# A segment sum by two matmul passes: a quarter of the late chunk products in two float32r parts

## The chip, the cores and the metric

The kernel runs on one core of one Trainium2 chip. The metric is the device time of one execution in microseconds (us), less is better. The core has five engines with a queue each: TensorE (PE in the profile, with its weight loads as PEld), VectorE (DVE), ScalarE (ACT), GpSimd (POOL) and SyncE (SP). Each engine works through its own queue in order. DMA transfers are started from the queues of SP, ACT and POOL.

## The reference, cut to what matters

```
def _L0_gnn_ref(x, edge_index, edge_features, global_feat, W_c, b_c, W1, b1, W2, b2, W3, b3):
    row = edge_index[0]
    edge_aggr = jnp.zeros((n, HIDDEN)).at[row].add(edge_features)
    combined = concatenate([x, edge_aggr, global_expand]) @ W_c + b_c
    h = softplus(combined @ W1 + b1)
    h = softplus(h @ W2 + b2)
    return h @ W3 + b3
x = layernorm(x + _L0_gnn_ref(x, stack([src, dst]), edge_attr_128, ...))
```

There are 206,250 edge rows of 128 float32 numbers and 6,250 nodes. An edge row is added to the row of its node `src`, and the `src` come in no order. The sum over the edges, `edge_aggr`, is nearly all of the work; the three small layers and the layer norm follow per node.

## The kernel before, in words

The sum is made in two passes over the edges, which run at the same time, the second behind the first.

- **Sort.** The nodes are cut into 32 buckets of 196 (`BL`). The edges lie in 1,692 columns of 122 rows, two columns make a pair (846 pairs), up to three pairs make a piece. For each column DVE and PE work out which place in its column each edge gets (`slot`), a 0/1 matrix `sort_hot` is made from it (every second piece by one comparison on DVE, L1137; the others on ACT by six `Abs`, L1140, and one `Relu`, L1142), PE multiplies the edge rows by it (`gather`, L1153, tile `sorted`), ACT copies the result out of PSUM (`settle`, L1165, tile `pairs`), and POOL writes each pair to its places in DRAM with one indirect DMA (`scatter_row`, L1182, tensor `rows_by`). Gaps between the places are filled with rows of -1 by DMAs from a tile `fill`.
- **Sum.** `rows_by` is read back in chunks of 128 rows, all of one bucket or of two neighbours. A load on SP's queue brings up to 8 chunks into one of 6 buffers (`chunks`). Its chunks are worked on in units of up to four (`HALF`). DVE makes a 0/1 matrix `hot` of 128 rows by 196 nodes for each chunk of a unit (`match`, L990), and PE multiplies the chunk's rows by it in float32 (`product`, L1013): the 128x128 rows are the weights, `hot` streams past them, and the result adds up in a PSUM tile `part`. When a group of chunks is through, DVE adds `part` to `sums_t` (L1036).
- **Node layers.** In 13 tiles of up to 512 nodes: PE L1356 and L1357 (first layer, from `x_t` and `sums_t`), ACT L1367, L1368, L1373 (softplus), DVE L1381, PE L1360 (second layer), PE L1395 (third), DVE L1403 to L1410 (sum with x and its statistics), then the norm.

The order on PE, DVE, ACT and SP is written out by a planner in the kernel. Every step gets a time in planned microseconds: pair k is scattered at `FIRST + SCATTER * k`, and its gather, settle, comparisons and loads lie fixed distances ahead (`GATHERED`, `SETTLED`, `COMPARED`, `LOADED`). `sum_steps` gives each unit the time of its match and of its product: a match may stand 2 units ahead of the products (`TOGETHER`), after the last scatter 4 (`AT_END`). Steps are then issued in order of these times. The planned end of the scatters is `ends[-1]`, 24 + 1.3 x 846 = 1123.8. Steps of the sum that are planned later than that are kept as `rest`, and the node layers take them in between their own steps: up to `FIRST_STEPS` = 9 of them ahead of a tile's second and third layer, those still needed for the next tile's first layer behind. I call what comes after the last scatter the tail.

A float32 matmul of this program stands in the profile as two MATMUL and two LDWEIGHTS: 1,758 chunks make 3,516 rows of L1013, and 1,692 columns 3,384 rows of L1153.

Of the kernel before, what the change touches and what calls it, by code (L numbers as in the profile page):

```python
# [7 lines left out]
F32 = mybir.dt.float32  # L8
BF16 = mybir.dt.bfloat16
# [5 lines left out]
ALU = mybir.AluOpType  # L15
# [36 lines left out]
FILL, DUE = 7, 8  # L52
# [11 lines left out]
SHARE, SPREAD = 2, 2.0  # L64
# [3 lines left out]
MATCHED, MULTIPLIED, RATE = 9.0, 1.5, 0.58  # L68
NODES = (3, 4)
# [77 lines left out]
def kernel(  # L147
# [144 lines left out]
    def sync_dma(out, in_):  # L292
        return nc.sync.dma_start(out, in_).ins
# [16 lines left out]
    hots = ctx.enter_context(tc.tile_pool(name="hots", bufs=6))  # L310
# [8 lines left out]
    with ExitStack() as phase:  # L319
        rows_p = phase.enter_context(tc.tile_pool(name="rows", bufs=ROWS))  # L320
        sort_p = phase.enter_context(tc.tile_pool(name="sort", bufs=3))
# [29 lines left out]
        def scratch(name):  # L351
            return per.tile([P, 4 * P], F32, name=name, bufs=1)
# [53 lines left out]
        def fill_rows():  # L406
# [10 lines left out]
            def some(due, b, n, lo, rows, k):  # L417
                to = rows_by.rearrange("(s j) c -> s j c", j=STRIDE * P)[b:b + n, lo:lo + rows * k, :]
                ins = sync_dma(to.rearrange("b (p k) c -> p b (k c)", k=k),
                               fill[:rows, :k * ROW].unsqueeze(1).to_broadcast([rows, n, k * ROW]))  # L420
                apart(ins, "direct", ["scatter"])
                fills.setdefault(due, []).append(ins)

            def doubtful(b, mixed):
                if mixed:
                    start, end, twice, room, per = ROOM * P, STRIDE * P, 2, MIXED_ROOM / 2, MIXED_PER
                else:
                    start, end, twice, room, per = 0, rooms[b] * P, 1, rooms[b], ROWS_PER[kind[b]]
                lo = start + twice * int(certain(mixed, gap_at, room, per))
                hi = end - twice * untouched(mixed, per)  # L430
                rows, k = min(((rows, -(-(hi - lo) // rows)) for rows in (96, 112, P)),
                              key=lambda e: (e[0] * e[1], -e[0]))
                assert k <= FILL and lo + rows * k <= end
                return lo, rows, k
# [451 lines left out]
        def sum_steps():  # L886
# [37 lines left out]
            chunks, hots_of, parts_of, met, begun = {}, {}, {}, {}, set()  # L924
# [54 lines left out]
            def match(n):  # L979
                j, a, e = units_of[n]  # L980
                hot = hots.tile([P, HALF, BL], F32, name="hot")
                hots_of[n] = hot
                q = a
                while q < e:
                    lo = hi = place_in(j, q)
                    step, m = 1, 1
                    while q + m < e and place_in(j, q + m) > hi and (m == 1 or place_in(j, q + m) == hi + step):
                        step, hi = place_in(j, q + m) - hi, place_in(j, q + m)
                        m += 1
                    nc.vector.tensor_tensor(  # L990
                        hot[:, q - a:q - a + m],
                        chunks[j][:, lo:hi + 1:step, D:W].to_broadcast([P, m, BL]),
                        iota_ps.unsqueeze(1).to_broadcast([P, m, BL]), op=ALU.is_equal)
                    q += m
# [3 lines left out]
            def product(n):  # L998
# [9 lines left out]
                for q in range(a, e):  # L1008
# [4 lines left out]
                    nc.tensor.matmul(part[:, b - base_of[v], :], t[:, place_in(j, q), :D], hot[:, q - a],  # L1013
                                     start=first, stop=last)
# [26 lines left out]
            opened = -1  # L1041
            for n, (j, a, e) in enumerate(units_of):
# [11 lines left out]
                found.append((match_at[n], len(found), lambda n=n: match(n)))  # L1054
                found.append((product_at[n], len(found), lambda n=n: product(n)))
# [561 lines left out]
```

## Time and profile before

| | |
|---|---|
| median of 3 runs | 1289.03 us (1283.15 to 1290.0) |
| the profiled execution | 1289.92 us, its span 1288.2 us |
| busy, of the span | PE 91%, PEld 86%, DVE 80%, ACT 78%, POOL 68% |
| scatters | 846, the first at 22.1 us, the last starts at 1127.05 us |
| TensorE clock granted, mean | 0.962 |

A row of the groups reads: line, engine, operation, output and inputs, partitions x elements, count | busy us, mean ns of one | idle time of the engine ahead of it, and what ended the idle time. A row of the timeline: start us, length us, engine, line, operation, count. A row of the windows: the stretch, then for each engine its busy us and in brackets the number of instructions. Matmuls overlap each other, so that the distance between two starts is what one of a series costs, not its mean length.

### The profile page before, as it was taken

The numbers are of one execution on the slowest core, as the hardware profiler recorded it, in microseconds if no ns is written. First come the engines' busy times: TensorE is split into PE (matmuls) and PEld (weight loads), VectorE is DVE, ScalarE is ACT, GpSimd is POOL, SyncE is SP. The second block draws the span as 40 slices with busy tenths as digits, with TensorE's granted clock in tenths as the row PEclk, the third lists the DMA queues.
The fourth block names the chain that finished last, engine by engine and source line by source line (L and its number), as shares of the span: only waits on it lengthen the run. The fifth ranks groups of instructions, "written<-read, shape, count | busy, mean of one in ns | idle before, by whom it ended". The sixth has DMA issues, their size and how long they took to land.

```text
span 1288.2 us, 26304 instructions
## 1 busy us (share of the span) xinstructions
PE 1167.7 (91%) x8617; PEld 1111.8 (86%) x8617; DVE 1027.6 (80%) x2260; ACT 1003.9 (78%) x2335; POOL 880.9 (68%) x915
## 2 busy tenths in 40 slices
PE   5778898888998998999899999999999999899893
PEld 5667788877988898989899999999999999898772
DVE  7868977888789977899878887789876767687784
ACT  5897987899687888977998888988899999403343
POOL 2777777777577776776777777777777777750334
PEclk9788998989999998999999999999999999999996
DMA  6789998899999997997999999999999999874421
GB/s 248 240 296 347 344 334 288 305 344 355 339 327 331 362 330 278 319 325 246 322 309 309 323 336 328 345 313 335 316 350 334 369 336 363 288 218 140 140 75 53
DMA packets 174636, 381.96 MB, mean 297 GB/s; under 512 B 27546, under 2 KB 118626, under 8 KB 160670
## 3 DMA queue, kind: packets, MB, share of 16 engines
q1 hardware_dynamic: 130751, 260.70, 61.2%
q0 software_dynamic: 41328, 115.65, 23.1%
q10 hardware_dynamic: 2415, 3.85, 0.9%
q8 instruction: 72, 1.18, 0.4%
q14 instruction: 70, 0.57, 0.1%
HBM read 242.47 MB, written 142.20 MB: 299 GB/s over the span
## 4 chain that ended last, share of the span: by engine, by line
PE 65%; DVE 12%; ACT 8%; DMA 7%; issue 4%; POOL 3%; SPq 0%; ACTq 0%; DVEq 0%; POOLq 0%
PE part L1013 37%; PE sorted L1153 21%; ACT pairs L1165 4%; DMA rows_by<-pairs,pair 4%; POOL rows_by L1182 3%; ACT sort_hot L1140 3%; DMA chunks<-rows_by 3%; DVE hot L990 2%; DVE past L727 1%; PE small L557 1%; PE small L559 1%; ACT sort_hot L1142 1%; DVE sort_hot L1137 1%; DVE sums_t L1036 1%; PE small L1395 1%
## 5 line engine op out<-in xcount | busy, mean ns | idle before, releaser
L1182 POOL DMA_INDIRECT rows_by<-pairs,pair x846 | 828.1, 979 | 298.3 <-issue 202.8
L1013 PE MATMUL part<-hot,chunks 128*128 128x196 f32 x3516 | 675.1, 335 | 13.2 <-DVE sums_t L1036 9.9
L1165 ACT COPY pairs<-sorted 64x387 f32<-64x387 f32 (+2 forms) x1144 | 542.6, 474 | 118.8 <-PE sorted L1153 95.7
L1013 PEld LDWEIGHTS part<-hot,chunks 128*128 128x128 f32 x3516 | 582.0, 193 | 21.9 <-DVE sums_t L1036 11.3
L1153 PE MATMUL sorted<-rows,sort_hot 122*128 122x129 f32 x3384 | 498.5, 288 | 44.5 <-ACT sort_hot L1142 32.0
L1153 PEld LDWEIGHTS sorted<-rows,sort_hot 122*128 122x128 f32 x3384 | 457.6, 199 | 53.5 <-ACT sort_hot L1142 36.3
L990 DVE TENSOR_TENSOR hot<-chunks,both_ps 128x784 f32<-128x784 f32 (+3 forms) x541 | 426.1, 809 | 9.2 <-DMA chunks<-rows_by 9.0
L1140 ACT ACTIVATE sort_hot<-plain,slot 122x128 f32<-122x128 f32 x840 | 292.8, 394 | 18.6 <-PE sorted L1153 6.3
L1036 DVE TENSOR_TENSOR sums_t<-sums_t,part 128x392 f32<-128x392 f32 (+1 forms) x262 | 143.5, 548 | 134.0 <-PE part L1013 133.0
L1137 DVE TENSOR_TENSOR sort_hot<-slot,both_ps 122x768 f32<-122x768 f32 x143 | 134.5, 940 | 1.9 <-PE sorted L1153 1.0
L1142 ACT ACTIVATE sort_hot<-sort_hot 122x768 f32<-122x768 f32 x143 | 118.6, 830 | 3.9
L1437 POOL TENSOR_SCALAR y<-y,mv,rs 128x128 f32<-128x128 f32 x40 | 31.1, 785 | 93.8 <-DVE rs L1425 93.5
L576 DVE TENSOR_REDUCE slot<-small 122x16 f32<-122x512 f32 (+2 forms) x109 | 72.9, 668 | 21.5 <-PE small L559 20.7
L1367 ACT ACTIVATE away<-sorted,z_bias 128x512 f32<-128x512 f32 (+2 forms) x13 | 8.5, 656 | 72.9 <-PE sorted L1357 72.9
L498 DVE TENSOR_TENSOR pair_ib<-pair_block,plain 122x512 bf16<-122x512 bf16 (+2 forms) x157 | 63.4, 411 | 0.2
L557 PE MATMUL small<-pair_ib,half 122*122 122x512 bf16 (+2 forms) x109 | 43.3, 398 | 7.6 <-DVE slot L576 7.5
L742 PEld LDWEIGHTS <-past 128*128 128x128 f16 x424 | 25.4, 100 | 17.9 <-DVE past L727 12.7
L727 DVE TENSOR_TENSOR past<-both_ps,starts 128x512 f16<-128x512 f32 (+1 forms) x61 | 39.8, 664 | 1.2 <-PE small L742 0.9
L742 PE MATMUL small<-jump,past 128*128 128x56 f16 (+3 forms) x424 | 29.4, 190 | 11.8 <-DVE past L727 8.4
L559 PEld LDWEIGHTS <-starts_h 128*122 128x122 bf16 x236 | 25.3, 148 | 11.9 <-issue 7.7
L1114 ACT COPY rows<-pair_i 122x16 f32<-122x16 f32 x106 | 22.2, 209 | 17.0 <-DMA rows<-in_edge 16.4
L727 DVE TENSOR_TENSOR past<-both_ps,starts_late 128x512 f16<-128x512 f32 (+2 forms) x49 | 32.3, 661 | 0.0
(163 smaller groups left out, 515.6 us busy)
## 6 DMA issues: line engine op xcount, KB each, us to landing
rows<-in_edge SPq DMA_DIRECT2D x105, 1032.0 KB
chunks<-rows_by SPq DMA_DIRECT2D x362, 136.0 KB
chunks<-rows_by SPq DMA_DIRECT2D x203, 204.0 KB
chunks<-rows_by SPq DMA_DIRECT2D x75, 272.0 KB
rows_by<-pairs,pair POOLq DMA_INDIRECT x846
rows_by<-fill SPq DMA_DIRECT2D x10, 1249.5 KB
rows_by<-fill SPq DMA_DIRECT2D x10, 714.0 KB
chunks<-rows_by SPq DMA_DIRECT2D x13, 408.0 KB
```

The costliest lines, as they stand in the source:

```text
L498: nc.vector.tensor_tensor(ib, cols.unsqueeze(2).to_broadcast([PN, m, SB, QUAD]), bucket_at[:PN].unsqueeze(1).to_broadcast([PN, m, SB, QUAD ...
L576: nc.vector.tensor_reduce(to, of, axis=mybir.AxisListType.X, op=ALU.max)
L727: nc.vector.tensor_tensor(past[:, :, a:b], twice_ps[:KB].unsqueeze(1).unsqueeze(1).to_broadcast([KB, 2, b - a, P // 2]), own["starts"][:, ...
L990: nc.vector.tensor_tensor(hot[:, q - a:q - a + m], chunks[j][:, lo:hi + 1:step, D:W].to_broadcast([P, m, BL]), iota_ps.unsqueeze(1).to_bro ...
L1013: nc.tensor.matmul(part[:, b - base_of[v], :], t[:, place_in(j, q), :D], hot[:, q - a], start=first, stop=last)
L1036: nc.vector.tensor_add(here, here, of)
L1137: return [lambda: nc.vector.tensor_tensor(hot[:PN, :2 * m], slot[:PN, at:at + 2 * m].unsqueeze(2).to_broadcast([PN, 2 * m, P]), slot_ps[:P ...
L1140: return [lambda j=j: nc.scalar.activation(hot[:PN, j], by_slot[:PN], AF.Abs, bias=slot[:PN, at + j:at + j + 1], scale=-1.0) for j in rang ...
L1142: for j in range(2 * m)] + [lambda: nc.scalar.activation(hot[:PN, :2 * m], hot[:PN, :2 * m], AF.Relu, bias=1.0, scale=-1.0)]
L1153: nc.tensor.matmul(out[:, j, :], hot[:PN, at], rows_at[col // LOAD_COLS][:PN, col % LOAD_COLS, :], start=True, stop=True)
L1165: nc.scalar.copy(sets_at[i][64 * n:64 * n + 64, lo:lo + m, h, :W], out[64 * h:64 * h + 64, :m, :])
L1182: s = nc.gpsimd.indirect_dma_start(out=dst, out_offset=bass.IndirectOffsetOnAxis(ap=at, axis=0), in_=rows[:, j].rearrange("p a b -> p (a b ...
```

## The change

- **Two float32r parts.** From planned time 650 on, every fourth unit (after the last scatter every third) that has more than two chunks, lies in one run of its load, and is not planned between 30 ahead of the last scatter and 12 behind it, becomes `fine`. ACT copies its rows into a tile `high` as float32r (`high`), 4 planned us ahead of the product; DVE subtracts that from the rows and writes the remainder over them as float32r (`low`), 1.5 ahead; and PE makes two float32r products for each chunk where one float32 product was, `high` by `hot` and remainder by `hot`. There are two buffers for `high`. 76 units with 266 chunks become fine: 55 units (185 chunks) ahead of the last `gather`, 21 units (81 chunks) behind it.
- **Comparisons earlier.** `SPREAD` goes from 2.0 to 4.5: the comparisons of the sort on ACT start 17.5 + 4.5 = 22 planned us ahead of the scatter instead of 19.5, and `sort_hot` gets 4 buffers instead of 3.
- **Room.** `hot` gets 5 buffers instead of 6. `fill` holds 4 rows instead of 7, so that 12 fills become two DMAs each, and the scratch tiles of `node_codes` are halved.

```
-FILL, DUE = 7, 8
+FILL, DUE = 4, 8
-SHARE, SPREAD = 2, 2.0
+SHARE, SPREAD = 2, 4.5
+FINE_FROM, FINE_EVERY, HIGHS, COARSE = 650.0, (4, 3), 2, (-30.0, 12.0)
-    hots = ctx.enter_context(tc.tile_pool(name="hots", bufs=6))
+    hots = ctx.enter_context(tc.tile_pool(name="hots", bufs=5))
-        sort_p = phase.enter_context(tc.tile_pool(name="sort", bufs=3))
+        sort_p = phase.enter_context(tc.tile_pool(name="sort", bufs=4))
...
+                for a in range(0, k, FILL):
+                    w = min(FILL, k - a) * ROW
+                    ins = sync_dma(to[:, :, a * ROW:a * ROW + w],
+                                   fill[:rows, :w].unsqueeze(1).to_broadcast([rows, n, w]))
...
+            def high(n):
+                high_of[n] = sums_p.tile([P, HALF, D], F32R, name="high", bufs=HIGHS)
+                for to, at, m in runs_of(n):
+                    nc.scalar.copy(high_of[n][:, to], chunks[units_of[n][0]][:, at, :D])
+
+            def low(n):
+                for to, at, m in runs_of(n):
+                    rows = chunks[units_of[n][0]][:, at, :D]
+                    nc.vector.tensor_tensor(rows.bitcast(F32R), rows, high_of[n][:, to].bitcast(F32),
+                                            op=ALU.subtract)
...
-                    nc.tensor.matmul(part[:, b - base_of[v], :], t[:, place_in(j, q), :D], hot[:, q - a],
-                                     start=first, stop=last)
+                    rows, by = t[:, place_in(j, q), :D], hot[:, q - a]
+                    if n in fine:
+                        nc.tensor.matmul(part[:, b - base_of[v], :], high_of[n][:, q - a], by,
+                                         start=first, stop=False)
+                        nc.tensor.matmul(part[:, b - base_of[v], :], rows.bitcast(F32R), by,
+                                         start=False, stop=last)
+                    else:
+                        nc.tensor.matmul(part[:, b - base_of[v], :], rows, by.bitcast(F32),
+                                         start=first, stop=last)
...
+                since += 1
+                if (product_at[n] > FINE_FROM and since >= FINE_EVERY[product_at[n] > ends[-1]]
+                        and not COARSE[0] < product_at[n] - ends[-1] < COARSE[1] and e - a > 2 and len(runs_of(n)) == 1):
+                    since = 0
+                    fine.add(n)
+                    found.append((max(match_at[n], product_at[n] - 4.0), len(found), lambda n=n: high(n)))
+                    found.append((max(match_at[n] + 1.0, product_at[n] - 1.5), len(found), lambda n=n: low(n)))
```

The times of the other steps in the plan stay as they were: 1,471 of the 1,758 chunk products stand ahead of the sort's last matmul on PE before and after.

PE in the tail, around the first tile that reaches its third layer (L1395). Before:

```order
L1356 MATMUL sorted<-x_t,fold 128x512
L1357 MATMUL sorted<-sums_t,fold 128x512
L1013 MATMUL part<-hot,chunks 128x196 x10
L1360 MATMUL sorted<-h_13613,weights_sb 128x512
L1395 MATMUL small<-weights_sb,h_13615 128x128 x4
L1013 MATMUL part<-hot,chunks 128x196 x14
```

The same place after the change (the lines have moved: L1042 is the float32 product, L1037 and L1039 are the two float32r products of a chunk):

```order
L1392 MATMUL sorted<-x_t,fold 128x512
L1393 MATMUL sorted<-sums_t,fold 128x512
L1042 MATMUL part<-hot,chunks 128x196 x10
L1396 MATMUL sorted<-h_14042,weights_sb 128x512
L1431 MATMUL small<-weights_sb,h_14044 128x128 x4
L1037 MATMUL part<-hot,high 128x196
L1039 MATMUL part<-hot,chunks 128x196
```

The first four of the 14 chunks behind the third layer are now a fine unit (the last two rows stand there four times), and the other ten follow it.

DVE at the same place, before:

```order
L1403 TENSOR_TENSOR y<-small,x_sb 128x512
L1406 BN_STATS stats<-y 128x6 x4
L1410 BN_AGGR mv<-stats 128x2 x4
L990 TENSOR_TENSOR hot<-chunks,both_ps 128x392 x2
L1036 TENSOR_TENSOR sums_t<-sums_t,part 128x392
```

And after (L1015 is the subtraction of `low`):

```order
L1439 TENSOR_TENSOR y<-small,x_sb 128x512
L1442 BN_STATS stats<-y 128x6 x4
L1446 BN_AGGR mv<-stats 128x2 x4
L1015 TENSOR_TENSOR chunks<-chunks,high 128x4x128
L1002 TENSOR_TENSOR hot<-chunks,both_ps 128x392 x2
L1065 TENSOR_TENSOR sums_t<-sums_t,part 128x392
```

The remainder of that unit stands behind the statistics of the tile, which wait for the third layer.

ACT in the sort, around copies into three of the six sets of pairs (111 to 113) that belong to planned times near 1000, before:

```order
L1165 COPY pairs_111<-sorted 64x3x129 x2
L1140 ACTIVATE sort_hot<-plain,slot 122x128
L1142 ACTIVATE sort_hot<-sort_hot 122x768
L1165 COPY pairs_112<-sorted 64x3x129 x4
L1140 ACTIVATE sort_hot<-plain,slot 122x128 x2
L1165 COPY pairs_113<-sorted 64x3x129 x2
```

And after (L1201 are the copies, L1176 and L1178 the comparisons, L1010 is `high`):

```order
L1178 ACTIVATE sort_hot<-sort_hot 122x768
L1201 COPY pairs_111<-sorted 64x3x129 x2
L1010 CAST high<-chunks 128x384
L1201 COPY pairs_112<-sorted 64x3x129 x2
L1176 ACTIVATE sort_hot<-plain,slot 122x128 x3
L1201 COPY pairs_112<-sorted 64x3x129 x2
```

The comparisons stand two copies earlier, and a copy into `high` has come between those of two sets.

35 lines of the change are left out of this document (20 added, 15 removed).

## The prediction

> **What bounds the kernel now.** I read the page's first and fourth part, then the windows, then the waits and the timeline of the engine that the fourth part does not name.
>
> ```profile
> span 1288.2 us, 26304 instructions
> PE 1167.7 (91%) x8617; PEld 1111.8 (86%) x8617; DVE 1027.6 (80%) x2260; ACT 1003.9 (78%) x2335; POOL 880.9 (68%) x915
> PE 65%; DVE 12%; ACT 8%; DMA 7%; issue 4%; POOL 3%; SPq 0%; ACTq 0%; DVEq 0%; POOLq 0%
> ```
>
> By these three lines it is PE's kernel. The windows of the scatter alone (L1182; POOL's busy us and count), and POOL's timeline in a quiet stretch, first and last of 13 rows, say something else:
>
> ```profile
> 22.00:128.00 106.00, 80.87 (x83) 0.87 0.82 286
> 128.00:614.00 486.00, 355.51 (x363) 0.96 0.92 322
> 614.00:1128.00 514.00, 391.68 (x402) 1.00 0.96 330
> ```
>
> ```profile
> 899.43 0.97 POOL L1182 DMA_INDIRECT rows_by<-pairs,pair  x1 [0.30 <-issue]
> ...
> 914.76 0.97 POOL L1182 DMA_INDIRECT rows_by<-pairs,pair  x1 [0.30 <-issue]
> ```
>
> Twelve distances in 15.33 us are 1.277 us a scatter: 0.97 busy and 0.30 ahead of each that nothing visible causes. 402 scatters at 1.277 are 513.4 us, and the window from 614 to 1128 has 514. There POOL goes at its own pace and loses 0.6 us in all. From 128 to 614, 363 x 1.277 = 463.6 of 486: 22.4 us lost. POOL's waits before 614, then behind it (us in total, times, longest):
>
> ```profile
> POOL rows_by L1182 <- DMA rows_by<-pairs,pair: 19.6, 34, 6.4
> POOL rows_by L1182 <- ACT pairs L1165: 16.6, 27, 2.1
> ```
>
> ```profile
> POOL rows_by L1182 <- issue: 93.7, 307, 0.3
> POOL rows_by L1182 <- ACT pairs L1165: 7.9, 25, 0.6
> ```
>
> Behind 614 a wait is 0.3 us long, which is the pace itself. So PE may be full there and still not set the end of the sort; the last scatter does, which starts at 1127.05. The tail behind it lasts 161 us. All engines by stage (us of the stage; PE, PEld, DVE, ACT, POOL busy):
>
> ```profile
> 650.00:900.00 250.00, 249.16 (x1879) 245.23 (x1878) 206.67 (x374) 218.79 (x514) 190.51 (x196) 1.00 0.95 326
> 900.00:1094.00 194.00, 193.65 (x1404) 192.59 (x1403) 141.26 (x213) 177.75 (x419) 147.63 (x153) 1.00 0.98 344
> 1128.00:1160.00 32.00, 32.00 (x177) 31.04 (x178) 26.81 (x43) 1.38 (x3) 15.47 (x16) 0.95 0.73 212
> 1160.00:1256.00 96.00, 88.86 (x451) 71.64 (x450) 74.95 (x176) 39.53 (x65) 22.17 (x30) 1.00 0.40 118
> ```
>
> In the tail to 1256, the last chunk product, PE is busy 120.9 of 128 us and DVE 101.8: PE is the bound there, DVE close behind.
>
> **The price of a float32r product.** No row has one. The nearest are the float32 and 16-bit matmuls of one stretch of PE's timeline, and a float32 one with few columns:
>
> ```profile
> 901.25 0.39 PE L559 MATMUL small<-half,starts_h_late 128*122 128x128 bf16 x4
> 901.48 1.55 PE L1013 MATMUL part<-hot,chunks 128*128 128x196 f32 x8
> 902.86 0.83 PE L1153 MATMUL sorted<-rows,sort_hot 122*128 122x129 f32 x6
> 903.53 0.27 PE L742 MATMUL small<-jump,past 128*128 128x56 f16 x4
> 903.64 0.92 PE L1153 MATMUL sorted<-rows,sort_hot 122*128 122x129 f32 x6
> 904.39 1.49 PE L1013 MATMUL part<-hot,chunks 128*128 128x196 f32 x8
> 905.72 0.50 PE L1153 MATMUL sorted<-rows,sort_hot 122*128 122x129 f32 x3
> ```
>
> ```profile
> 658.63 0.55 PE L620 MATMUL small<-earlier_late,plain 128*128 128x62 f32 x4
> 659.02 0.44 PE L1153 MATMUL sorted<-rows,sort_hot 122*128 122x129 f32 x2
> ```
>
> By start to start, L1013 takes 1.33 / 8 = 0.166 an instruction, 0.333 a chunk: 0.85 ns for each of its 196 columns. L559 takes 0.23 / 4 = 0.058, 0.45 ns for each of 128: half. So a float32 instruction passes its columns at half rate, and one pass of 196 is some 0.083. But weights count too. L620 has 62 columns and takes 0.39 / 4 = 0.098 where its columns at 0.85 ns would take 0.053: loading 128 float32 weights holds a matmul to about 0.1, and L1153 (0.67 / 6 = 0.112, 129 columns) fits that as well. L742 with 16-bit weights takes 0.11 / 4 = 0.028. So a float32r product lies between 0.083 (weights as fast as 16-bit ones) and 0.166 (columns at the rate of float32), or, if it is made like a whole float32 product, 0.333. I take 0.112, the load of 4-byte weights, because its weights are 4 bytes wide as in L620 and L1153. A fine chunk then costs 0.223 for 0.333 and saves 0.11; the ends are 0.167 saved, none, and 0.333 lost.
>
> The Trainium skill has the rule in "TensorE: Matmul & The Clock Gate", LDWEIGHTS: a load takes its columns over 1.2 GHz, 107 ns for 128, as L620's 0.098 roughly shows. The same page, Weight-path perf modes, gives a faster load to 128 weights whose type is not FP32, and does not say which side float32r is on; by that the saving would be 0.167.
>
> **Where that counts.** Ahead of 1128: 55 units, 185 chunks, 185 x 0.11 = 20 us of PE. POOL is at its pace from 614 on, so they bring nothing to the end; the cover that makes them worthless is the 1.277 of the scatter. In the tail, 81 chunks x 0.11 = 8.9 us of PE, on the path.
>
> **What it adds.** One `high` on ACT and one `low` on DVE for each unit. The nearest rows:
>
> ```profile
> L1368 ACT ACTIVATE away<-away 128x512 f32<-128x512 f32 x22 | 13.9, 630 | 0.7
> L1368 ACT ACTIVATE away<-away 128x370 f32<-128x370 f32 x2 | 1.0, 512 | 0.1
> L1381 DVE SCALAR_TENSOR_TENSOR h<-sorted,neg_b,away 128x512 f32<-128x512 f32 x11 | 8.2, 742 | 1.6 <-ACT away L1373 1.6
> L990 DVE TENSOR_TENSOR hot<-chunks,both_ps 128x392 f32<-128x392 f32 x81 | 42.6, 553 | 0.0
> ```
>
> `high`: 0.63 for four chunks, 0.52 for three. `low`: 0.66 for four, between the 0.553 for 392 numbers and the 0.742 for 512 with an operand in PSUM; 0.54 for three.
> - ACT in the sort: 55 units, 20 of four chunks and 35 of three, 12.6 + 18.2 = 31 us on 396.5 busy of 444 (650 to 1094): 96%. From 900 on about half of them, 15 us on 177.75 of 194, 99%. Part of ACT's idle time is waiting for PE, which is relieved by some 10 us there; I cost it at nothing, and name the case where it is not as a rival.
> - DVE in the sort: 20 x 0.66 + 35 x 0.54 = 32 us on 348 of 444: 86%. Hidden.
> - DVE in the tail: 21 units, 18 of four and 3 of three, 13.5 us on 101.8 of 128. It fits (115), but not everywhere. Its idle time is waiting for the third layer, and PE already waits for DVE in places:
>
> ```profile
> DVE y L1403 <- PE small L1395: 15.5, 9, 2.6
> PE part L1013 <- DVE sums_t L1036: 5.7, 3, 3.5
> ```
>
>   I put 3 of the added `low`s into such places: 2 us.
> - PE behind a `low`. At the place of the first order above, the fine unit stands directly behind the third layer. Its `low` stands on DVE behind that tile's statistics. Before:
>
> ```profile
> 1177.39 1.05 PE L1395 MATMUL small<-weights_sb,h 128*128 128x128 f32 x8
> 1178.28 3.48 PE L1013 MATMUL part<-hot,chunks 128*128 128x196 f32 x20
> 1178.55 0.69 DVE L1403 TENSOR_TENSOR y<-small,x_sb 128x512 f32<-128x512 f32 x1 [2.58 <-PE small L1395]
> 1180.07 0.36 DVE L1410 BATCH_NORM_AGGREGATE mv<-stats 128x2 f32<-128x6 f32 x4
> 1184.58 0.30 PEld L1357 LDWEIGHTS sorted<-sums_t,fold 128*128 128x128 f32 x2 [1.06 <-DVE sums_t L1036]
> ```
>
>   Here PE goes on at 1178.28. With the `low` it goes on when DVE is through at 1180.43 and 0.66 later: 1181.1, 2.8 us late. The wait of 1.06 at this tile's end goes away for that, and the rest is the loss, some 1.7. One more tile has the same order (products, third layer, fine unit, with `low` behind the statistics): 3 us for both. ACT's queue agrees: `high` there stands behind a softplus, which ends about when the statistics do.
>
> Sum of the tail: -8.9 + 2 + 3 = -3.9 us.
>
> **The small edits.** Earlier comparisons: PE waited for them, 23 times in the whole span:
>
> ```profile
> PE sorted L1153 <- ACT sort_hot L1142: 32.0, 23, 2.2
> ```
>
> Only what lies before 614 can count. POOL's loss there that comes through ACT's copies is 16.6 less 27 x 0.3 = 8.5 us, and this edit can reach only the part that begins with a late comparison; on the other side a comparison moved ahead delays one copy by up to 1 us where POOL has no lead. Between -8.5 and +2 I take -2. The split fills: 12 more issues on SP and the same bytes, between 250 and 440 us, where POOL loses more to DMA; bounded by +3 and by the gain of about as much if shorter packets let scatters through, taken as 0. One `hot` buffer less: the plan uses 4 ahead in the tail, 5 suffice: 0.
>
> The sum: 1289.9 of the profiled execution - 3.9 - 2 = 1284.0. That execution lies 0.9 above the median of 1289.03; I leave the 0.9 in the range.
>
> **The rivals.**
> - *Weights of float32r load like 16-bit ones.* L742 shows that PE can. 0.166 a chunk, 81 x 0.167 = 13.5 us; DVE at 115 of 114.5 us would then be the bound of the tail, which takes back some: 1280. It is what the Trainium skill's faster load (the section named above) would do here, if float32r does not count as FP32.
> - *Columns at float32's rate* (ends on the other side): 0.166 a product, a fine chunk costs the 0.333 it did. It decides from 0.136 a product on, where PE's saving, 81 x (0.333 - 2 x 0.136) = 5 us, no longer covers the 5 us of waits. The `low`s then stand on a path that got nothing: +5 in the tail, and up to 5 in the sort, where ACT at 99% meets a PE without relief: 1293 to 1300, say 1296. For it: the 4-byte columns of L1013 do pass at half rate; against it: that is also what two passes for each column would look like.
> - *ACT becomes the sort's bound.* Place: 900 to 1094. Price: ACT's 193 of 194 us leave nothing for its waits on PE; if these stay (about 10 us there) POOL stands 10 less whatever lead its sets hold, 5 or so: 1289 to 1294.
> - *The early stretch recovers.* If the 8.5 us on ACT's copies go and a few of the DMA's 19.6 - 34 x 0.3 = 9.4: -10 in place of -2: 1276.
> - *A float32r product of so few columns is made as a float32 one*, 0.333: 81 x 0.333 = 27 us in the tail and 62 on a full PE in the sort: about 1375.
>
> **How the numbers follow.** My forecast has 42%, its own range 1278 to 1291 (from no tail cost beyond one of the terms to none of the early gain and 4 more of waits). Fast weights 20%, columns at float32's rate 13%, ACT as the bound 12%, the early recovery 8%, the slow product 5%. Less than 0.5% (6.4 us, below 1282.6 or above 1295.5) is about what a measurement of this kernel can't tell from no change; its three runs span 6.9. Faster: two fifths of the forecast, three quarters of the fast weights, all of the early recovery: 40%. Slower: two thirds of the third case, a quarter of ACT's, the slow product, and a little of the forecast: 20%. The same: 40%. The range, 1271 to 1299, leaves out the slow product and the ends of the others.
>
> **What the profile after would show.** Rows of L1037 and L1039 at 0.112 start to start: the price is right; 0.083 or 0.166 are the rivals. 1.277 us a scatter from 614 to the last one, with PE now idle some 20 us there: the relief is worthless. PE waiting 2 to 3 us for L1015 in the tail, and the tail 157 us long in place of 161. Wrong it would be above all by the price, and by POOL waiting for L1201 behind 900.

## The result and the profile after

The changed kernel takes 1306.48 us (median of 6 runs, 1301.89 to 1307.65), the kernel before 1287.18 beside it (6 runs): 1.0148 times as long, 95% interval 1.0123 to 1.0172. That is 19.3 us more where 5 less were forecast.

Span, busy time and the chain of waits of the kernel after, the same three lines of the page that were shown of before:

```profile
span 1303.9 us, 26601 instructions
PE 1155.7 (89%) x8617; PEld 1089.1 (84%) x8617; DVE 1077.5 (83%) x2336; ACT 1018.3 (78%) x2411; POOL 885.2 (68%) x915
PE 42%; DMA 19%; DVE 17%; ACT 9%; issue 7%; POOL 5%; SPq 1%; ACTq 0%; DVEq 0%; POOLq 0%
```

PE has 12 us less work, and the span is 15.7 longer. Where, the windows tell. The first fence has the scatter alone (L1218), the second all engines in the two parts of the tail:

```profile
128.00:614.00 486.00, 361.98 (x369) 0.96 0.94 326
```

```profile
1128.00:1160.00 32.00, 19.46 (x104) 18.18 (x102) 28.68 (x30) 2.77 (x5) 11.49 (x12) 0.78 0.36 104
1160.00:1256.00 96.00, 83.30 (x430) 68.15 (x431) 79.58 (x171) 39.38 (x66) 16.19 (x21) 0.95 0.44 128
```

The sort is not longer in this execution: 369 scatters began between 128 and 614 where 363 did, and the last one of all starts at 1122.61 instead of 1127.05. The tail is: from there to the end 181.3 us instead of 161.2. In its first 32 us PE was full before; now it is busy 19.46, at a granted clock of 0.78. What PE waited for from 1123 on (us in total, times, longest), and the timeline of the place:

```profile
PE part L1039 <- DVE chunks L1015: 20.0, 7, 11.0
```

```profile
1122.61 0.97 POOL L1218 DMA_INDIRECT rows_by<-pairs,pair  x1 [0.30 <-issue]
1123.67 15.82 POOL L1492 TENSOR_TENSOR x_sb<-x_sb,b_all 128x512 f32<-128x512 f32 x15
1126.43 12.75 DVE L1015 TENSOR_TENSOR chunks<-chunks,high 128x512 fp32r<-128x512 f32 x1
...
1139.24 0.53 PE L1039 MATMUL part<-hot,chunks 128*128 128x196 f32 x1 [10.96 <-DVE chunks L1015]
```

One `low` (L1015) is on DVE for 12.75 us. It starts 2.8 us into POOL's block of 15 additions of b3 to the rows of x, which follows the last scatter, and ends 0.3 us ahead of that block's end. Of all 76 the shortest, median and longest (ns):

```profile
L1015 DVE TENSOR_TENSOR chunks<-chunks,high x76: 546/614/12754, 659.7 to 1264.5; 128x512 fp32r<-128x512 f32 x38, 128x384 fp32r<-128x384 f32 x38
```

The granted clock (the number behind POOL's) falls while PE waits, and for ten microseconds after:

```profile
1123.00:1140.00 17.00, 6.04 (x21) 5.68 (x20) 15.75 (x7) 1.17 (x2) 16.40 (x16) 0.60 0.46 141
1140.00:1150.00 10.00, 9.62 (x47) 9.23 (x47) 6.99 (x12) 1.13 (x3) 0.00 (x0) 0.72 0.32 88
```

In the kernel before it was 0.87 from 1127 to 1140 and 1.00 in the ten microseconds behind.

Theory T from this: DVE reads both operands of `low` in SBUF, POOL's additions read SBUF too, and DVE is locked out until they are through. Rival Q: the tail is long because `high` and `low` stand in queues, and the 12.75 us is something of the first use. Rival S: part of the loss comes from the sort.

### The profile page after: what moved, and what is told of

Read it like the earlier page. It is cut to its first block, busy times and chain, and to the rows that moved or that the text cites. A ratio compares the mean times of both kernels' runs of the same rounds, so it can differ in the third digit from the quotient of the medians.

```text
span 1303.9 us, 26601 instructions
## 1 busy us (share of the span) xinstructions
PE 1155.7 (89%) x8617; PEld 1089.1 (84%) x8617; DVE 1077.5 (83%) x2336; ACT 1018.3 (78%) x2411; POOL 885.2 (68%) x915
## 4 chain that ended last, share of the span: by engine, by line
PE 42%; DMA 19%; DVE 17%; ACT 9%; issue 7%; POOL 5%; SPq 1%; ACTq 0%; DVEq 0%; POOLq 0%
PE part L1042 20%; PE sorted L1189 13%; DMA rows_by<-pairs,pair 9%; DMA chunks<-rows_by 7%; POOL rows_by L1218 5%; ACT pairs L1201 5%; DVE hot L1002 4%; ACT sort_hot L1176 3%; PE part L1039 2%; DVE chunks L1015 2%; DMA rows_by<-fill 2%; PE part L1037 1%; DVE past L732 1%; DVE sums_t L1065 1%; DVE sort_hot L1173 1%
## 5 line engine op out<-in xcount | busy, mean ns | idle before, releaser
L1218 POOL DMA_INDIRECT rows_by<-pairs,pair x846 | 831.2, 983 | 291.1 <-issue 201.8
L1201 ACT COPY pairs<-sorted 64x387 f32<-64x387 f32 (+2 forms) x1144 | 542.7, 474 | 125.9 <-PE sorted L1189 81.7
L1042 PE MATMUL part<-hot,chunks 128*128 128x196 f32 x2984 | 586.0, 339 | 12.2 <-DVE sums_t L1065 8.8
L1189 PE MATMUL sorted<-rows,sort_hot 122*128 122x129 f32 x3384 | 497.5, 287 | 45.5 <-ACT pairs L1201 38.8
L1042 PEld LDWEIGHTS part<-hot,chunks 128*128 128x128 f32 x2984 | 500.8, 195 | 17.6 <-DVE sums_t L1065 9.6
L1189 PEld LDWEIGHTS sorted<-rows,sort_hot 122*128 122x128 f32 x3384 | 450.2, 197 | 60.1 <-ACT pairs L1201 52.4
L1002 DVE TENSOR_TENSOR hot<-chunks,both_ps 128x784 f32<-128x784 f32 (+5 forms) x541 | 427.7, 810 | 7.9 <-PE part L1042 3.5
L1176 ACT ACTIVATE sort_hot<-plain,slot 122x128 f32<-122x128 f32 x840 | 281.0, 392 | 9.5 <-DVE slot L581 6.0
L1178 ACT ACTIVATE sort_hot<-sort_hot 122x768 f32<-122x768 f32 x143 | 118.4, 828 | 0.4
L1473 POOL TENSOR_SCALAR y<-y,mv,rs 128x128 f32<-128x128 f32 x40 | 32.2, 812 | 112.6 <-DVE rs L1461 112.3
L1010 ACT CAST high<-chunks 128x512 fp32r<-128x512 f32 (+1 forms) x76 | 42.2, 558 | 71.2 <-PE part L1037 25.7
L1039 PE MATMUL part<-hot,chunks 128*128 128x196 f32 x266 | 66.5, 286 | 24.4 <-DVE chunks L1015 24.0
L1039 PEld LDWEIGHTS part<-hot,chunks 128*128 128x128 f32 x266 | 51.7, 194 | 30.0 <-DVE chunks L1015 28.0
L1037 PE MATMUL part<-hot,high 128*128 128x196 f32 x266 | 73.4, 307 | 3.0 <-DVE sums_t L1065 3.0
L1015 DVE TENSOR_TENSOR chunks<-chunks,high 128x512 fp32r<-128x512 f32 (+1 forms) x76 | 59.0, 777 | 11.4 <-ACT high L1010 11.4
L1037 PEld LDWEIGHTS part<-hot,high 128*128 128x128 f32 x266 | 51.9, 195 | 5.3 <-issue 4.9
```

What stands on the lines that cost most here:

```text
L1002: nc.vector.tensor_tensor((hot if n in fine else hot.bitcast(F32))[:, to], chunks[j][:, at, D:W].to_broadcast([P, m, BL]), iota_ps.unsquee ...
L1015: nc.vector.tensor_tensor(rows.bitcast(F32R), rows, high_of[n][:, to].bitcast(F32), op=ALU.subtract)
L1037: nc.tensor.matmul(part[:, b - base_of[v], :], high_of[n][:, q - a], by, start=first, stop=False)
L1039: nc.tensor.matmul(part[:, b - base_of[v], :], rows.bitcast(F32R), by, start=False, stop=last)
L1042: nc.tensor.matmul(part[:, b - base_of[v], :], rows, by.bitcast(F32), start=first, stop=last)
L1176: return [lambda j=j: nc.scalar.activation(hot[:PN, j], by_slot[:PN], AF.Abs, bias=slot[:PN, at + j:at + j + 1], scale=-1.0) for j in rang ...
```

## The experiments

Each was timed in five rounds beside the kernel before. Medians in us; the ratio is to the kernel before of the same series (1286.7 to 1287.3, but for one pair of series named below). "Products" is the time from the start of the last scatter to the start of the last ten chunk products, in the profiled execution: 129.1 before, 149.3 after. It is one execution's figure: the profiled ones of "parts in the sort only" (1289.60), "first parts 30 us behind" (1299.71), "SPREAD 2.0" (1283.56) and "products in float32" (1280.55) lie 4.8 and 6.1 us above and 4.8 and 3.5 below their medians.

| kernel | median | ratio, 95% interval | products |
|---|---|---|---|
| no additions of b3 on POOL | 1291.25 | 1.0032, 1.0020 to 1.0043 | 132.6 |
| parts in the sort only | 1284.76 | 0.9984, 0.9966 to 1.0002 | 127.0 |
| no parts | 1284.40 | 0.9985, 0.9969 to 1.0001 | 129.8 |
| parts in the tail only | 1302.37 | 1.0118, 1.0100 to 1.0137 | 146.4 |
| first parts 30 us behind the scatters | 1293.63 | 1.0050, 1.0031 to 1.0069 | 141.7 |
| seven additions instead of 15 | 1297.26 | 1.0088, 1.0067 to 1.0109 | 141.5 |
| 30 us, and parts made earlier | 1284.83 | 0.9987, 0.9974 to 1.0000 | 127.2 |
| 30 us, `low` of the tail on POOL | 1302.27 | 1.0119, 1.0097 to 1.0140 | 146.8 |
| tail only, 45 us, made earlier | 1277.33 | 0.9931, 0.9909 to 0.9952 | 123.4 |
| the same, products in float32 | 1284.08 | 0.9971, 0.9955 to 0.9988 | 127.8 |
| no parts, SPREAD 2.0 | 1288.35 | 1.0008, 0.9992 to 1.0024 | 128.1 |

**Without POOL's additions.**

```
-                for lo, hi, r in blocks_of(w):
-                    nc.gpsimd.tensor_tensor(
-                        x_of[n0][:r, lo:hi, :], x_of[n0][:r, lo:hi, :],
-                        b3_all[:r].unsqueeze(1).to_broadcast([r, hi - lo, D]), op=ALU.add)
```

> This kernel leaves out the 15 additions of b3 to the rows of x on POOL at the start of the tail (x_sb<-x_sb,b_all, 15.82 us in a row in the changed kernel), so b3 is missing from its result; nothing else differs from the changed kernel, and the order on PE, DVE and ACT is the same. Theory T (the first low of the tail, 12.75 us instead of 0.61, was locked out by these POOL additions, and the clock fell while PE waited 10.96 us): that low takes about 0.6 us, PE's long wait goes, the granted clock in the first 30 us of the tail stays near 0.95, and the time is 1290 to 1295 us, 11 to 16 below the changed kernel. Rival Q (the tail is long because high and low are made in queues behind other work of ACT and DVE, and the 12.75 us is a slow first use or a wait for a buffer): the low stays long or another wait takes its place, and the time is 1302 us or more.

1291.25, 15.2 below the changed kernel: T's number. The first `low` of the tail, on the same place in DVE's order:

```profile
1127.76 0.68 DVE L1015 TENSOR_TENSOR chunks<-chunks,high 128x512 fp32r<-128x512 f32 x1
1128.50 0.42 PE L1039 MATMUL part<-hot,chunks 128*128 128x196 f32 x1 [0.29 <-DVE chunks L1015]
```

0.68 us, and PE waits 0.29 for it. The granted clock is 0.93 in the first 20 us of the tail and 0.91 in the next 40, a little under the 0.95 that T named. And the kernel is still 6.9 us slower than the one with no parts at all (next but one). In the two profiled executions 4.7 of that lies ahead of the last scatter (it starts at 1124.82 instead of 1120.15; more on it below), and 2.8 between it and the last chunk products, where PE should have gained. PE's waits name what eats that gain:

```profile
PE part L1039 <- DVE chunks L1015: 10.0, 8, 2.5
```

**Half of the additions.**

```
-                for lo, hi, r in blocks_of(w):
+                for lo, hi, r in blocks_of(w) if n0 <= tiles[6][0] else ():
```

> This kernel leaves out the additions of b3 to x for all tiles but the first seven, so that POOL's block of additions is 7 x 1.26 = 8.8 us long instead of 15.8; b3 is missing from the rest of the result. Theory T (the low is held until POOL's whole block is over): the first low of the tail ends with the seventh addition and takes 5.5 to 6.8 us, and the time is 1297 to 1301 us, between the 1291 without additions and the 1306 with all. Rival P (DVE and POOL share the port by turns, each at half its pace): the low takes about 1.3 to 2.6 us whatever stands behind it. Rival Q: 12.7 us as before.

```profile
1123.22 8.59 POOL L1492 TENSOR_TENSOR x_sb<-x_sb,b_all 128x512 f32<-128x512 f32 x7
1126.06 6.30 DVE L1015 TENSOR_TENSOR chunks<-chunks,high 128x512 fp32r<-128x512 f32 x1
1132.42 0.53 PE L1039 MATMUL part<-hot,chunks 128*128 128x196 f32 x1 [4.65 <-DVE chunks L1015]
```

POOL ends at 1131.81, the `low` 0.55 later, a little less than the 0.68 that it takes undisturbed. Its 6.30 us are T's number and neither P's 1.3 to 2.6 nor Q's 12.7; the time, 1297.3, lies between those without additions and with all. How long the `low` is held is set by POOL's block.

**Parts in the sort only, in the tail only, nowhere.**

```
-                if (product_at[n] > FINE_FROM and since >= ...
+                if (FINE_FROM < product_at[n] <= ends[-1] and since >= ...    (sort only)
-FINE_FROM, ... = 650.0, ...
+FINE_FROM, ... = 1123.8, ...    (tail only)
+FINE_FROM, ... = 1e9, ...    (nowhere)
```

> Two-part products only in the sort, none after the last scatter; the tail is that of the kernel before, with the rest of the change kept. Theory T: the whole loss is the tail's, so this is 1282 to 1285 us, 2 to 5 below the kernel before (the last scatter starts 4.4 us earlier in the changed kernel), and equal within 2 us to the kernel without any parts, since POOL's pace of 1.277 us hides whatever PE gains in the sort. Rival S (the parts cost something in the sort too, a lower clock or ACT running late into the tail): slower than the kernel without parts by over 3 us.

> Two-part products only after the last scatter, at the same units or nearly as in the changed kernel; none in the sort. Theory T: as slow as the changed kernel, 1302 to 1308 us, with one low of over 10 us while POOL adds b3 to the rows of x. Rival S (part of the loss comes from the sort, through the clock or through late work): 1295 us or less.

> No product in two parts at all: what is left of the change is the comparisons started 4.5 instead of 2.0 scatters apart from the plan, four buffers instead of three for the sort, five hots instead of six, smaller scratch and the fills cut at 4. Theory T: these alone bring the last scatter 4 to 5 us earlier and the time to 1281 to 1285 us, with a tail of 161 us as before. Rival S: 1287 us as before, the earlier end of the scatters being due to PE's relief in the sort.

Sort only and nowhere are equal within the uncertainty (1284.76, 1284.40). But the traces show that this is two effects that cancel, and not none. Behind 650, where the parts begin, POOL gets fewer scatters into the same time. The scatter alone, sort only, then nowhere:

```profile
650.00:1110.00 460.00, 351.85 (x356) 1.00 0.95 328
```

```profile
650.00:1110.00 460.00, 350.65 (x360) 1.00 0.96 331
```

None of POOL's waits there is over 0.3 us; some scatters themselves are longer. One of sort only, with the `low` beside it:

```profile
942.16 0.68 DVE L1015 TENSOR_TENSOR chunks<-chunks,high 128x512 fp32r<-128x512 f32 x1
942.27 1.42 POOL L1218 DMA_INDIRECT rows_by<-pairs,pair  x1 [0.30 <-issue]
```

In that trace 23 scatters begin while a `low` runs; they last 1.17 us on average, all others 0.98. Beginning during a comparison into `hot` or an addition to `sums_t`, which have an operand in PSUM, they last 0.98 too (171 and 50 cases). So a `low` holds up POOL's scatters, the very thing that sets the pace. The longest scatter from 650 to 1110 takes 1.35 to 1.49 us in all eight profiled kernels of this pace with parts in the sort and 1.15 to 1.21 in the five with SPREAD 4.5 and none, and the last scatter starts at 1122.2 to 1128.7 and at 1119.0 to 1121.5. That is about 3 us between the middle values, one execution of each kernel. By the longer scatters alone it is 23 x 0.19 = 4.4 us in sort only, and 2.2 to 5.6 in the eight. Against it stands a shorter tail, as PE's relief would give: behind the last scatter the products take 127.0 us instead of 129.8. No run takes the `low`s alone out of the sort, so both prices are read from the traces and not tested.

Tail only has nearly the whole loss, with a `low` of 11.90 us. That it is 4.1 us faster than the changed kernel, S's sign with a smaller size, T did not expect; more on it below.

**The first parts later.** COARSE ends 30 instead of 12 us behind the planned end of the scatters.

> One constant of the changed kernel is moved: no unit is made in two parts within 30 instead of 12 us (as planned) after the planned end of the scatters, so that the first low comes when POOL's 15 additions of b3 are over. All is computed. Theory T: no low takes over 0.8 us, PE's wait of 11 us is gone, and the time is 1289 to 1293 us (the kernel without the additions had 1291.2, and has four more such units in the tail). Rival Q (a long first low or a long wait comes wherever the first part in the tail stands): 1300 us or more.

The order was moved too little:

```profile
1125.26 15.74 POOL L1492 TENSOR_TENSOR x_sb<-x_sb,b_all 128x512 f32<-128x512 f32 x15
1137.09 3.60 DVE L1015 TENSOR_TENSOR chunks<-chunks,high 128x384 fp32r<-128x384 f32 x1
```

The first `low` still met the last 3.9 us of the block and took 3.60. The time, 1293.63, is above T's range by 0.6 us: the hold is shorter, not gone.

**The parts made earlier in the tail.**

```
-  max(match_at[n], product_at[n] - 4.0)          ... high(n)
-  max(match_at[n] + 1.0, product_at[n] - 1.5)    ... low(n)
+  max(match_at[n], product_at[n] - (9.0 if product_at[n] > ends[-1] else 4.0))         ... high(n)
+  max(match_at[n] + 1.0, product_at[n] - (5.0 if product_at[n] > ends[-1] else 1.5))   ... low(n)
```

> As the kernel with no parts within 30 us of the end of the scatters, and in the tail high is planned 9 instead of 4 us and low 5 instead of 1.5 us ahead of the products, which puts the lows ahead of y and the statistics in DVE's order (L1015 before L1439). Theory U (without the lock the tail's gain of 0.11 us per product on PE is lost in PE's waits for low behind y and the statistics, 10.0 us in 8 waits in the kernel without the additions): these waits fall under 3 us and the time is 1282 to 1287 us, 4 to 8 below the kernel with lows 1.5 us ahead. Rival V (DVE, 16 of 20 us busy, is the tail's bound, and 17 lows of 0.68 us lengthen it wherever they stand): the waits for low go and waits for hot, sums_t or h grow as much; 1289 to 1293 us.

8.8 us less than with the lows 1.5 us ahead, as U has it. PE's waits for `low` go from 11.7 us in five to one of 1.5, behind a `low` that POOL's block still held for 3.28 (before: a wait of 3.56 behind one of 3.60). V has a part of it: PE's waits for `sums_t` grow from 8.3 to 12.4 us. This is the second cause: where the `low` stands in DVE's order. A unit of the changed kernel that comes right after the third layer:

```profile
1188.89 1.05 PE L1431 MATMUL small<-weights_sb,h 128*128 128x128 f32 x8
1190.05 0.69 DVE L1439 TENSOR_TENSOR y<-small,x_sb 128x512 f32<-128x512 f32 x1 [2.25 <-PE small L1431]
1190.78 0.87 DVE L1442 BATCH_NORM_STATS2 stats<-y 128x6 f32<-128x128 f32 x4
1191.57 0.36 DVE L1446 BATCH_NORM_AGGREGATE mv<-stats 128x2 f32<-128x6 f32 x4
1191.85 0.66 DVE L1015 TENSOR_TENSOR chunks<-chunks,high 128x512 fp32r<-128x512 f32 x1
1192.56 0.36 PE L1039 MATMUL part<-hot,chunks 128*128 128x196 f32 x1 [2.52 <-DVE chunks L1015]
```

DVE first waits 2.25 us for PE's third layer, then does y and the statistics, and only then `low`; PE has gone on to the unit and waits 2.52. With the parts made earlier `low` is ahead of y at such a place, and DVE's wait for the third layer (2.05 us at the first such tile) comes only behind it. The kernel is no faster than the one with no parts (1284.83, 1284.40): its products behind the last scatter take 127.2 us instead of 129.8, and its last scatter starts at 1123.00 instead of 1120.15.

**`low` on POOL.** `nc.vector` becomes `nc.gpsimd` in `low` for the tail's units.

> As the kernel with no parts within 30 us of the end of the scatters, but the lows of the tail run on POOL, which is idle for most of it (6.5 of 20 us busy), at the 1.26 us of POOL's 128x512 additions, in place of 0.68 us on DVE. Theory V (DVE's time is the bound): DVE is relieved of 17 x 0.68 = 11.6 us, and if the wait for a slower low on POOL stays under 1 us each the time is 1282 to 1287 us. Theory U: PE waits longer for each low, which starts only after high and takes twice as long, behind norm work in POOL's order: 1290 to 1296 us. If POOL's reads of two SBUF operands hold up DVE's own work, y or h take over 1 us and the time is over 1296.

1302.27, above the 1290 to 1296 that U gave it, and not through DVE being held up: no y takes over 0.69 us there and no h over 0.75. PE's waits, two of the three:

```profile
1215.62 0.53 PE L1039 MATMUL part<-hot,chunks 128*128 128x196 f32 x1 [8.84 <-POOL chunks L1015]
1252.89 0.53 PE L1039 MATMUL part<-hot,chunks 128*128 128x196 f32 x1 [8.94 <-POOL chunks L1015]
```

Each is a `low` behind 12 normalizations in POOL's order (L1473, 3.91 + 3.11 + 2.34 us and what lies between), which themselves waited for DVE. POOL is idle for most of the tail and still the wrong engine: its idle time is waiting, with the `low` queued behind.

**Tail only, early, away from POOL's block.** FINE_FROM 1123.8 and COARSE up to 45 us, on top of the earlier places: 15 units of four products. Then the same kernel with both parts made but one float32 product in place of the two.

> Two-part products in the tail alone, none within 45 us of the planned end of the scatters (so that no low meets POOL's additions), high planned 9 and low 5 us ahead: 15 units of four products. All is computed. Theory U (on PE each unit saves 4 x 0.11 = 0.44 us, 6.6 us in all, once no low is late): 1278 to 1281 us, 4 to 6 below the kernel without parts (1284.4). Theory V (DVE's 15 x 0.68 = 10.2 us are paid back at the waits for hot, sums_t and h): 1283 to 1287 us, no better than without parts.

> As the kernel with 15 units in two parts in the tail made 9 and 5 us ahead, and ACT and DVE make both parts at the same places, but PE multiplies them as before, with one float32 product of 0.166 us a pass in place of two float32r products; the high part is left out of those products. It measures what the making of the parts costs by itself, without PE's gain. Theory U (DVE's work is hidden): 1284 to 1286 us, as without parts. Theory V: 1287 to 1292 us, 3 to 7 us above the kernel without parts, about what PE gains.

1277.33, better than both kernels, 10 us below the kernel before and 0.7 below U's range. All of its lows are of one length, and `low` is gone from PE's waits (from 1120 on):

```profile
L1015 DVE TENSOR_TENSOR chunks<-chunks,high x15: 679/683/685, 1141.4 to 1235.6; 128x512 fp32r<-128x512 f32 x15
```

```profile
PE part L1037 <- DVE sums_t L1065: 5.5, 4, 1.9
PE sorted L1396 <- DVE h L1417: 3.7, 2, 2.5
PE small L1431 <- DVE h L1417: 3.3, 1, 3.3
PE sorted L1393 <- DVE sums_t L1065: 1.6, 2, 1.0
PE part L1042 <- PE part L1042: 0.7, 2, 0.4
```

With float32 products the time is 1284.08, as with no parts. So making the parts costs nothing that can be told here (U; V falls). The float32r products are worth 6.75 us by the medians and about 5 by the two ratios, each of them uncertain by 2 to 3: 0.09 to 0.11 for each of the 60 chunks, against the 0.11 of PE's timeline.

**No parts, SPREAD back at 2.0.**

> No product in two parts, and SPREAD back at 2.0: of the change only the fourth buffer of the sort, five hots, smaller scratch and the fills cut at 4 are left. The prediction put 2 us on SPREAD. If so: 1286 to 1288 us, as the kernel before, where SPREAD 4.5 gave 1284.4. If the gain is the fourth buffer's: 1284 to 1285 us.

1288.35 against 1284.40 with 4.5, in another series: 4 us by the medians, 3 by the ratios, whose intervals just overlap. So the small edits' gain is SPREAD's as far as the runs can tell, and the buffers and the cut fills are worth nothing that can be told (ratio 1.0008, 0.9992 to 1.0024).

**Parts in the sort beside early parts in the tail.** FINE_FROM back at 650.

> The kernel with 15 units in two parts in the tail made 9 and 5 us ahead (1277.3), and besides these the changed kernel's parts in the sort. What is open: parts in the sort cost nothing when they were alone (1284.8 against 1284.4 without), but the changed kernel was 4.1 us slower than the one with parts in the tail alone (1306.5 against 1302.4). If the parts of the sort cost nothing, 1276 to 1279 us. If they cost something (ACT's highs, or a clock that PE gets after the sort), 1280 to 1283 us, and the last scatter comes later or the granted clock in the tail is lower.

> The same kernel as the one before (15 units in two parts in the tail made 9 and 5 us ahead, and the changed kernel's parts in the sort), once more, because the kernel before itself had 1598 us in that series instead of 1287. If the parts of the sort cost nothing, 1276 to 1279 us; if they cost something, 1280 to 1283 us.

> The kernel with 15 units in two parts in the tail alone, on the same chip as the one with parts in both, for a comparison between the two: 1276 to 1279 us again. The difference between the two is the price of the parts in the sort: 0 by the runs with parts in the sort alone, 4 us by the runs of the changed kernel and of the one with parts in the tail alone.

> Parts in both the sort and the tail (9 and 5 us ahead, none near POOL's additions), a third time, since in the last two series the kernel before had 1598 and 1619 us and PE waited for its own instructions there. On a chip where the kernel before has 1287 us: 1276 to 1279 us if the parts of the sort cost nothing, 1280 to 1283 us if they cost something.

> Parts in the tail alone, beside the kernel with parts in both on the same chip: 1276 to 1279 us on a chip where the kernel before has 1287 us.

In the first two series the kernel before itself had 1598 and 1619 us. There POOL waits for ACT's copies, which wait for PE (198.5 us for L1189), and the pace of the scatters no longer covers PE (POOL's waits in the tail-only kernel, whole span):

```profile
POOL rows_by L1218 <- ACT pairs L1201: 346.7, 143, 6.8
```

These series say nothing on the kernel bound by 1.277 us a scatter, and in them the best version is not better than the kernel before (1620.74; 1.0021, 0.9990 to 1.0052), the one with parts in both slower (1606.47 and 1627.37; 1.0056 and 1.0061, both intervals above 1). In the third series: 1280.52 with parts in the sort (0.9955, 0.9938 to 0.9971), 1278.51 without (0.9932, 0.9911 to 0.9952). The 2 us between them can't be told from nothing, as the intervals overlap. The traces have the two effects again: the last scatter starts 3.7 us later with parts in the sort (1123.17, 1119.50), and the products behind it take 2.5 less (121.3, 123.9).

## Why the prediction was wrong

- *POOL's pace sets the sort's end* held, but not that the parts leave the pace alone. From 614 to 1128 none of POOL's waits for `high` and ACT's copies is over 0.3 us, so ACT did not become the bound. DVE's lows in the sort, called "Hidden", lengthen the scatters that begin beside them, about 3 us by the last one; the tail is 2.5 to 2.8 us shorter in the two pairs compared, which the prediction's worthless relief of PE would explain. That sort only equals no parts, as forecast, is by these readings two effects that cancel, and so in part luck.
- *The price of a float32r product* held. PE's timeline in the changed kernel:

```profile
956.52 0.27 PE L1039 MATMUL part<-hot,chunks 128*128 128x196 f32 x1
956.63 0.28 PE L1037 MATMUL part<-hot,high 128*128 128x196 f32 x1
956.74 0.27 PE L1039 MATMUL part<-hot,chunks 128*128 128x196 f32 x1
```

  0.11 from start to start, which rules out 0.083 and 0.166. That it is the load of 4-byte weights is argued from L620 and L1153, no run varies it. The 8.9 us on the tail's 81 chunks were there to be had: 60 of them gave 5 to 7.
- *What it adds* is the step that failed. `low` was priced 0.66 "between the 0.553 ... and the 0.742", from two rows that read one operand in PSUM, and taken to be that long wherever it stands ("It fits"). The row of 1128 to 1160 quoted there had POOL busy for 15.47 us, and what POOL does then was not asked. In the kernel before that block disturbed nobody: DVE's instructions beside it have an operand in PSUM and take their usual time (0.56 us for a sums_t of 392 at 1132.56, 0.97 for a hot of 784 at 1130.76). `low` is the first one there with both in SBUF. It is held for 12.75 us instead of 0.68. That POOL's block does this is shown by leaving out the additions and by halving them. That the two operands in SBUF are the reason no run tests, as none has a `low` with an operand in PSUM. But the profile before already had a sign of it, in the other direction: its `pair_ib` (L498), too, is a DVE instruction with both operands in SBUF, and a scatter that begins while one runs is longer:

```profile
272.14 0.42 DVE L498 TENSOR_TENSOR pair_ib<-pair_block,plain 122x512 bf16<-122x512 bf16 x1
272.22 1.18 POOL L1182 DMA_INDIRECT rows_by<-pairs,pair  x1 [0.30 <-ACT sort_hot L1142]
```

  The 30 such scatters last 1.05 us on average, the 233 that begin during a `hot` (L990) and the 72 during a `sums_t` (L1036) 0.97. The Trainium skill states the rule in "SBUF — State Buffer", Who interferes with whom: a DVE instruction with two SBUF inputs contends with a GpSimd instruction that reads SBUF, and the loser stands still. The trace agrees that `low` stands still. That section also says that the order of issue decides who blocks; here `low` waited through twelve instructions of POOL, eleven of them begun after it, and beside POOL's normalizations, begun before it, it did not wait (last section). The price of POOL's block by removal is 15.2 us: PE's wait of 11.0, of which 0.3 is left without the additions, and about 4.5 more, for which the profile offers the clock of 0.72 that follows (there a float32r product takes 0.21 instead of 0.11); no run has the wait without the clock.
- *PE behind a `low`, 3 us* was mis-sized. The two tiles named wait 2.52 each where 2.8 was said, but six other units wait as well: 10.0 us in 8 waits once the additions are gone. The waits that were to go in exchange, like the one of 1.06, hardly did: the first layer's products wait 2.2 us for sums_t, 2.4 before.
- *DVE's lows, 2 us*: nothing. Without the additions PE's waits in the tail for `sums_t` and h sum to 15.9 us, 15.7 in the kernel before.
- *The small edits, -2*: -2.4 against the kernel before by the medians, with an interval that just reaches no change, and 3 to 4 for SPREAD alone. Cut fills and one `hot` less at 0 held.
- No rival had `low` held by POOL. Those that ended slower (the price of the columns, ACT as the bound, the slow product) had other mechanisms.

The account: no parts 1284.4; parts as in the changed kernel but with no additions on POOL 1291.25; the additions bring 1306.5. Of the first step, in the profiled executions, 4.7 us lie ahead of the last scatter, about what the scatters that begin during a `low` are longer in that trace (32 of them, 1.12 us for 0.98), and 2.8 behind it, where -8.9 of PE meets 10 of waits and a granted clock of 0.91 to 0.93 in the first 60 us of the tail (0.91, 1.00 and 1.00 before). The second step is the hold and what follows it.

Why the changed kernel is 4.1 us slower than the one with parts in the tail alone can be followed in the two traces, which differ by 4.1 us as well. Its last scatter starts 1.15 later; it has the parts in the sort. From there both go alike for the first 39 us: the `low`, though held 0.85 longer, ends 16.57 and 16.58 behind the last scatter's start. Then the changed kernel loses 2.95, nearly all in two places where its granted clock falls to 0.66 (1162.61 to 1167.61 and 1247.61 to 1252.61) and the other's stands at 1.00. Why the clock falls there in the one and not in the other stays open; one of the changed kernel's six runs, at its highest mean clock of 0.964, took 1301.89.

## What to carry to other kernels

Before an instruction is added, look at what the other engines do in each place where it will stand, and at where each of its operands lies: a price taken from instructions with an operand in PSUM did not hold here for one with both in SBUF beside POOL's additions, and it delayed POOL's scatters in turn. An instruction that feeds the bounding engine belongs ahead of the waits of its own engine's queue; `high` 5 and `low` 3.5 us earlier in the plan were worth 8.8 us here, some 2 of them from meeting less of POOL's block. And an engine whose idle time is waiting in order (POOL here) is no free engine.

## What the hardware showed that was not expected

POOL's additions follow each other without a gap, and `low` did not get in between two of them. It waited out twelve in a row, though each is an instruction of its own, of 1.26 us mostly, and got in only ahead of the last. That one then took longer; the page's groups of the last addition, first after, then before:

```profile
L1492 POOL TENSOR_TENSOR x_sb<-x_sb,b_all 114x128 f32<-114x128 f32 x1 | 0.9, 892 | 0.0
```

```profile
L1456 POOL TENSOR_TENSOR x_sb<-x_sb,b_all 114x128 f32<-114x128 f32 x1 | 0.4, 445 | 0.0
```

0.89 instead of 0.45: there POOL waited for DVE in turn. The same stands in all four kernels with the full block and a `low` beside it on DVE (0.76 for a `low` of three chunks). Why DVE gets in at that place and not sooner stays open.

It is not so beside every instruction of POOL. The normalizations (L1473) follow each other without a gap as well and read SBUF too, but there `low` takes its usual 0.68 (0.76 at most in the other traces), and it is POOL's next one that is longer than its usual 0.78. In the changed kernel:

```profile
1224.31 0.68 DVE L1015 TENSOR_TENSOR chunks<-chunks,high 128x512 fp32r<-128x512 f32 x1
...
1224.55 1.11 POOL L1473 TENSOR_SCALAR y<-y,mv,rs 128x128 f32<-128x128 f32 x1
```

The additions read two tensors (x_sb and b_all), the normalizations one and two numbers for each row; no run tests whether that makes the difference.
